# A two-layer SCNN block: the fourth group's rows of layer 1 move between the two column scans, and the hand-over from rows to columns goes from tile to tile

## The chip, the cores and the metric

The kernel runs on one core of a Trainium2 chip. The metric is device time in microseconds (us) of one execution; a time "of the kernel" below is the median of three executions.

## The reference

The input `x` is an image batch of shape (32, 48, 64, 128): 32 images, 48 channels, 64 rows, 128 columns, all in f32. There are two layers, and each adds a scan to its input: `x = x + scnn(groupnorm(x))`. The normalization takes 16 groups of 3 channels per image. The scan is a spatial recurrence in four directions, one after another:

```python
def step(w, b):                       # w: 48 x 48 channels x 5 taps
    def f(carry, inp):
        nxt = inp + conv1d(carry, w, b)    # padding 2, along the line
        return nxt, nxt
    return f
# D: down the 64 rows (carry = a row of 128 columns), weights down_w
# U: up the rows of D, again with down_w
# R: right over the 128 columns of U (carry = a column of 64 rows), right_w
# L: left over the columns of R, left_w
```

A step needs the whole result of the step before it, so 2 x 63 row steps and 2 x 127 column steps of one image can't be done at the same time. Only different images are independent.

## The kernel before

**Tiling.** The 32 images are four groups of eight. A *row phase* runs the down and up scans of one group: 63 + 63 steps. A *column phase* runs the right and left scans of a *pair* of groups: 127 + 127 steps. With two layers there are eight row phases and four column phases, 2024 steps. TensorE runs them strictly one after another, in the order of the list `PHASES`; each entry is (kind, layer, group or pair), and k is a phase's place in the list, counted from 0. Before the change the end of the list is rows of layer 1 for groups 1, 2 and 3, then columns of layer 1 for pair 0 and for pair 1.

A step (function `step`, line 741) is nine 128x128 matmuls into three PSUM banks, and after each bank an add on VectorE (line 750) that puts bias and input to it and writes the new row or column into SBUF. The tiles of a step are named step_, layer, group or pair, and way: step_10r is layer 1, pair 0, right; step_13d is layer 1, group 3, down. A phase is called 10r, 13d and so on below.

**Memory.** SBUF holds an `arena` with three slots and four *stage* tiles, and a region `early` with weights. A row phase uses two slots (rows 0 to 31 and 32 to 63); which two alternates with the phase's number. A column phase works in quarters of 32 columns, three at a time: quarter 0 is spilled to DRAM after use and comes back for the left scan, and quarter 3 takes its place (`spill_unit`). Two more tiles, `spare_tiles`, lie on the region `early`, the first of them on the down weights.

**Two layouts.** In a row phase a partition is (column modulo 8, channel), in a column phase it is (row modulo 8, channel); both in three sets of 128. Going from rows to columns is a transposition between partitions. It is done by way of DRAM: `move_rows` writes rows to the buffers `ups` (line 589, in the trace `upa` and `upb` by layer), and `load_unit` (line 231's `dma`) reads them column-wise. Where a column phase comes straight after the row phase of its pair's second group, the last rows are on the critical path: this is called a *seam* (`follows`). There are two seams before the change: rows 01 to columns 00 and rows 03 to columns 01. At a seam the rows 0 and 1, which are finished last, are written and read separately, the reads on GpSimd's queue. `hold_queues` (the tile `pin`) makes SyncE's and ScalarE's queues wait until the first column is taken, so that the loads of the second quarter come behind.

**Row phases.** `plan_rows` loads a group's 64 rows in four batches of 16, and applies the normalization to each (`scale_rows`: 24 activations on ScalarE, line 614). Both have times of their own; behind a column phase the loads start 28, 12 steps before and 4, 20 steps after the phase's first step, the scalings 13 before and 3, 19, 35 after.

**Results of layer 1.** In the left scan a finished quarter's six units are handled one by one in `plan_cols`: the residual is loaded into a tile (`load_residual`, from the DRAM buffer `mid`, on ScalarE's queue), added on GpSimd (line 673), permuted by GpSimd and ScalarE (lines 569 and 698), and stored. Quarters 3 to 0 follow in this order. The results of the first pair's quarters 2, 1 and 0 (`HELD`) are first kept in DRAM (`hold_result`, ScalarE's queue) and later moved to the output (`let_result`, SyncE's queue). The residual for result n+2 into the tile of result n-2 (with four tiles) is issued after result n's copies:

```python
if u >= 2 and u - 2 + n < len(direct):
    at(t + 4.6, load_residual, k, *direct[u - 2 + n][1:], tiles[(u - 2) % n])
```

**The order is written by hand.** `at(t, fn, ...)` puts a call on an agenda at a time t counted in steps; `in_order` ties the instructions so that each engine keeps that order. DMAs go out on the queues of SyncE, ScalarE and GpSimd, each in order: an instruction that waits holds up all that stands behind it on its engine. The DMAs of SyncE and ScalarE share eight semaphores in turn, so that a DMA may also wait until the one eight before it in the program, on either queue, has landed.

Of the kernel before, what the change touches and what calls it, by code (L numbers as in the profile page):

```python
# [43 lines left out]
E8 = 8  # L44
FULL = 128
NG = E8 * C // FULL
NQ = 4
# [31 lines left out]
def weight_runs():  # L79
# [31 lines left out]
    ("cols", 0, 1),  # L111
    ("rows", 1, 1),
    ("rows", 1, 2),
    ("rows", 1, 3),
    ("cols", 1, 0),
    ("cols", 1, 1),
)

# [2 lines left out]
def kernel(  # L121
# [8 lines left out]
    nc = tc.nc  # L130
    B, _, H, W = x.shape
# [5 lines left out]
    RUN = KQ * GB  # L137
# [34 lines left out]
    spare_tiles = [early[:, i * UNIT : (i + 1) * UNIT] for i in range(2)]  # L172
# [38 lines left out]
        for half in range(2)  # L211
    }

    def by_row(t, e, h0, h1):


        t = t.rearrange("c (i q a e n) -> e a c i q n", i=E8, q=NQ, a=NH, e=E8)[e, h0 // E8]
        return t[:, h0 % E8 : h0 % E8 + h1 - h0].rearrange("c i q n -> c (i q) n")

    def lines(t, h0, h1):  # L220

# [8 lines left out]
    def dma(dst, src, queue=None):  # L230
        (queue or nc.sync).dma_start(dst, src)

    tail = {}

    def in_order(fn, *args):


        traced = nc.cur_bb.bb.instructions
        n = len(traced)
        fn(*args)  # L240
        for ins in traced[n:]:
            if ins.engine in tail:
                tc.add_manual_dep(
                    ins,
                    tail[ins.engine].name,
                    mybir.DependencyInfo(
                        mybir.DependencyClass.NoSync, mybir.DependencyReason.DATA
                    ),
                    reason="in_order",
                )  # L250
            tail[ins.engine] = ins

    def pieces(o):
# [332 lines left out]
    def row(k, h):  # L586
        return row_views(k)[h // HALF][:, :, h % HALF]

    def move_rows(k, h0, h1, to_dram):

        _, layer, g = PHASES[k]
        view = row_views(k)[h0 // HALF]
        t = (ups if to_dram else source)[layer][g]
        for h in range(h0, h1, E8):
            end = min(h1, h + E8)
            for o in range(NG):
                for e, c0, c1, p0 in pieces(o):
                    here = view[p0 : p0 + c1 - c0, o, h % HALF : h % HALF + end - h]
                    here = here.rearrange("p h (q n) -> p (h q) n", q=NQ)
                    there = by_row(t, e, h, end)[c0:c1]  # L600
                    if to_dram:
                        dma(there, here)
                    else:
                        dma(here, there)
# [25 lines left out]
    def quarter(k, j):  # L630
        return slot[slots(k)[j % 3]].rearrange("p (o s n) -> p s o n", s=2, o=NG)

    def load_unit(k, j, i, a0=0, a1=NH, e0=0, e1=E8, queue=None):


        _, layer, pair = PHASES[k]
        o, half = UNITS[i]
        part = slice(a0 * LINE, a1 * LINE)
        for e, c0, c1, p0 in pieces(o):
            if not e0 <= e < e1:  # L640
                continue
            dma(
                quarter(k, j)[p0 : p0 + c1 - c0, half, o, part],
                by_col(ups[layer][2 * pair + half], e, j)[c0:c1, part],
                queue,
            )

    def hold_queues(k):

# [170 lines left out]
    def at(t, fn, *args):  # L820
        agenda.append((t, len(agenda), fn, args))
# [31 lines left out]
    def plan_rows(k, t0, prev):  # L853
        if k == 1:
            ahead, scaled = (-34, -18, -3, 12), (-12, -2, 17, 33)
        elif prev == "cols":
            ahead, scaled = (-28, -12, 4, 20), (-13, 3, 19, 35)
        else:
            ahead, scaled = (-54, -43, 0, 11), (-22, -8, 16, 30)
        if k:  # L860
            for i in range(4):
                at(t0 + ahead[i], move_rows, k, i * LOAD, (i + 1) * LOAD, False)
                at(t0 + scaled[i], scale_rows, k, i * LOAD, (i + 1) * LOAD)

        cuts = list(range(0, H + 1, E8))
        following = PHASES[k + 1][0] == "cols"
        if following and follows(k + 1):
            cuts = [0, E8 // 4] + cuts[1:]
        for h0, h1 in zip(cuts, cuts[1:]):
            t = t0 + 2 * (H - 1) - h0  # L870
            if k == 0:
                t += 16 if h0 >= HALF else 68
            elif not following:
                t = t0 + 92 + 5 * (H - h1) / E8 + (34 if h1 <= HALF else 0)
            at(t, move_rows, k, h0, h1, True)
        at(
            t0 + H - 1,
            nc.gpsimd.tensor_copy,
            last.rearrange("p (o n) -> p o n", o=NG),
            row(k, H - 1),  # L880
        )

    def follows(k):

        _, layer, pair = PHASES[k]
        return PHASES[k - 1] == ("rows", layer, 2 * pair + 1)

    def plan_cols(k, t0, prev):
        _, layer, pair = PHASES[k]
        n = 2 * NG  # L890
# [3 lines left out]
        for i in range(n):  # L894
            if follows(k) and UNITS[i][1] == 1:
                other = nc.gpsimd
                at(t0 - 31 + i, load_unit, k, 0, i, 4, NH, 0, E8, other)
                at(t0 - 13 + i, load_unit, k, 0, i, 2, 4, 0, E8, other)
                at(t0 - 6 + i / n, load_unit, k, 0, i, 1, 2, 0, E8, other)
                at(t0 - 1.5, load_unit, k, 0, i, 0, 1, E8 // 4, E8, other)  # L900
                at(t0, load_unit, k, 0, i, 0, 1, 0, E8 // 4, other)
            else:
                early = 30 if after else 46 if k == 2 else 70
                at(t0 - early + 2 * i, load_unit, k, 0, i)
            if follows(k):
                queue = nc.scalar if i % 2 else nc.sync
                at(t0 + 1.5, load_unit, k, 1, i, 0, NH, 0, E8, queue)
            else:
                at(t0 + (3 if after else -24 + 2 * i), load_unit, k, 1, i)
            at(t0 + (38 if after else 8) + 2 * i, load_unit, k, 2, i)  # L910
            at(t0 + 33 + 2 * i, spill_unit, k, i, False)
            at(t0 + 50 + 2 * i, load_unit, k, 3, i)
        final = k == len(PHASES) - 1
        left = t0 + W - 1
        end = left + W - 1
        for i in range(n):

            t = left + 64 + 2 * i if layer == 0 else left + 39.5 + 4.5 * i
# [8 lines left out]
        if layer == 0:  # L927
            stats = ResultStatsV(f"r{2 * pair}"), ResultStatsA(f"r{2 * pair + 1}")
        tiles = [stage[:, i] for i in range(4)]
        if layer:  # L930
            tiles += spare_tiles[0 : 2 if final else 1]
        n = len(tiles)
        direct = [u for u in units if not (final and u[1] == 0)]

        for u, (t, j, i) in enumerate(direct):
            nat = tiles[u % n]
            o, half = UNITS[i]
            if u < n:
                soon = layer and u < 5
                at(left - 44 + 4 * u if soon else left + 16, load_residual, k, j, i, nat)  # L940
            if layer == 0:
                if u >= n:
                    at(direct[u - n][0] + 3, load_residual, k, j, i, nat)
                at(t, add_residual, k, j, i, nat)
                at(t + 4, keep_result, k, j, i)
                unit = quarter(k, j)[:, half, o]
                if half == 0:
                    for b in range(GB):
                        at(t + 5 + b, stats[0].take, j, o, unit, b)
                else:  # L950
                    at(t + 1, stats[1].take, j, o, unit)
            else:

                at(t, add_residual, k, j, i, nat)
                at(t + 2.5, permute_unit, k, j, i, nat, (nc.gpsimd, nc.scalar, nc.scalar))
                if final or j not in HELD:
                    at(t + 4.5, store_result, k, j, i, nat)
                else:
                    at(t + 4.5, hold_result, j, i, nat)
                if final and j == 1:  # L960
                    at(t + 4.7, load_residual, k, 0, i, last_tiles(k)[i])

                if u >= 2 and u - 2 + n < len(direct):
                    at(t + 4.6, load_residual, k, *direct[u - 2 + n][1:], tiles[(u - 2) % n])
        if layer == 0:
            t = units[-1][0] + 14
# [6 lines left out]
        if layer and not final:  # L973
            todo = [(j, half, e) for j in HELD for half in range(2) for e in range(E8)]
            for n, what in enumerate(todo):
                at(end + 63 + 1.9 * n, let_result, *what)
        if final:
            at(end + 4, last_results, k)

# [230 lines left out]
```

## Time and profile before

| | |
|---|---|
| runs of the kernel | 4333.52, 4343.96, 4350.06 us; median 4343.96 |
| profiled execution, own time | 4343.96 us; its span 4342.2 us |
| PE (TensorE) busy | 4066.5 us, 94% of the span, 36648 matmuls |
| DVE (VectorE) busy | 2165.5 us, 50% |
| ACT (ScalarE) busy | 1340.3 us, 31% |
| POOL (GpSimd) busy | 885.6 us, 20% |
| DMA | 680.12 MB, mean 157 GB/s |

"Busy" is the time in which an engine had an instruction at work; register, wait and DMA-issuing instructions are not counted. In a group's line the columns are: the source line, engine, operation, output and input with their shapes, the number of instructions, and behind the bar the busy time in us, the mean of one in ns, and the idle time of the engine just before them with what ended most of it. "PEclk" or "granted clock" is TensorE's clock as a share of full speed. In DMA lines the columns are the number of issues, the size of each and the median time from issue to landing.

### The profile page before, as it was taken

What the parts mean: (1) busy time and instruction counts of PE and PEld (TensorE: products, weight loads), DVE (VectorE), ACT (ScalarE), POOL (GpSimd) and SP (SyncE); (2) the same over time, 40 slices, a digit from 0 to 9 for tenths busy, and PEclk for the clock granted to TensorE, in tenths of its full rate; (3) what the DMA queues carried; (4) which work ended last, traced back from release to release, by engine and by line L of the source; (5) the groups of instructions that cost most, each with busy time, mean ns of one, the idle gap of its engine ahead of it and who ended that gap; (6) DMA issues with size and microseconds to landing.
All of it is one profiled execution on the core that took longest, in us unless ns stands there. A gap on an engine that the chain in (4) does not pass through costs nothing. (4 is left out here: it accounts for less than half of the span.)

```text
span 4342.2 us, 89984 instructions
## 1 busy us (share of the span) xinstructions
PE 4066.5 (94%) x36648; PEld 4036.5 (93%) x36648; DVE 2165.5 (50%) x6503; ACT 1340.3 (31%) x2662; POOL 885.6 (20%) x906
## 2 busy tenths in 40 slices
PE   3799998999999999989999999999997999989993
PEld 1699998999999999989999999999997999989992
DVE  6345444446654444444447654444443444444443
ACT  1584301526783556000006855403000002210122
POOL 4271011325323020010013410000000014520352
PEclk9899999999999999999999999999998999999996
DMA  8589799848999979579218979759049409999999
GB/s 211 112 215 163 108 163 188 224 112 242 221 181 163 157 148 154 95 125 225 48 27 272 199 144 156 108 90 179 3 67 179 118 13 244 247 250 167 156 211 182
DMA packets 2116733, 680.12 MB, mean 157 GB/s; under 512 B 2005440, under 2 KB 2056160, under 8 KB 2076384
## 3 DMA queue, kind: packets, MB, share of 16 engines
q1 hardware_dynamic: 2015904, 581.64, 69.2%
q10 hardware_dynamic: 97216, 86.44, 9.5%
q0 software_dynamic: 3200, 6.30, 0.6%
q8 instruction: 288, 4.72, 0.5%
q14 instruction: 125, 1.02, 0.1%
HBM read 397.38 MB, written 295.98 MB: 160 GB/s over the span
## 5 line engine op out<-in xcount | busy, mean ns | idle before, releaser
L614 ACT ACTIVATE arena<-arena,offset,scale 128x256 f32<-128x256 f32 (+2 forms) x816 | 575.7, 798 | 439.5 <-PE step_12u L741 116.8
L673 POOL TENSOR_TENSOR arena<-arena 128x2048 f32<-128x2048 f32 x80 | 363.0, 4553 | 1437.0 <-PE step_10l L741 501.6
L569 POOL COPY arena<-arena 96x256 f32<-96x256 f32 x448 | 264.8, 644 | 555.2 <-DMA arena<-in_x 445.4
L741 PE MATMUL step_10r<-arena,early 128*128 128x128 f32 x2286 | 254.0, 275 | 37.7 <-DVE arena L750 29.0
L741 PEld LDWEIGHTS step_10r<-arena,early 128*128 128x128 f32 x2286 | 253.6, 187 | 38.0 <-DVE arena L750 29.2
L512 ACT ACTIVATE early<-arena 128x256 f32<-128x256 f32 x192 | 129.6, 675 | 482.0 <-DMA arena<-xin 319.5
L741 PE MATMUL step_11r<-arena,early 128*128 128x128 f32 x2286 | 251.5, 274 | 15.2 <-DVE arena L750 15.2
L741 PEld LDWEIGHTS step_11r<-arena,early 128*128 128x128 f32 x2286 | 251.0, 185 | 15.6 <-DVE arena L750 15.6
L741 PE MATMUL step_01r<-arena,early 128*128 128x128 f32 x2286 | 251.1, 274 | 14.5 <-DMA arena<-upa 14.5
L741 PEld LDWEIGHTS step_01r<-arena,early 128*128 128x128 f32 x2286 | 250.9, 185 | 14.8 <-issue 14.7
L741 PE MATMUL step_00r<-arena,early 128*128 128x128 f32 x2286 | 250.9, 273 | 14.5 <-DMA arena<-upa 14.5
L741 PEld LDWEIGHTS step_00r<-arena,early 128*128 128x128 f32 x2286 | 250.6, 185 | 14.8 <-issue 14.8
L741 PE MATMUL step_00l<-arena,wleft 128*128 128x128 f32 x2286 | 249.1, 272 | 0.0
L741 PEld LDWEIGHTS step_00l<-arena,wleft 128*128 128x128 f32 x2286 | 248.6, 184 | 0.0
L741 PE MATMUL step_10l<-arena,wleft 128*128 128x128 f32 x2286 | 248.5, 272 | 0.0
L741 PE MATMUL step_11l<-arena,wleft 128*128 128x128 f32 x2286 | 248.5, 272 | 0.0
L741 PE MATMUL step_01l<-arena,wleft 128*128 128x128 f32 x2286 | 248.4, 272 | 0.0
L741 PEld LDWEIGHTS step_10l<-arena,wleft 128*128 128x128 f32 x2286 | 248.4, 184 | 0.0
L741 PEld LDWEIGHTS step_11l<-arena,wleft 128*128 128x128 f32 x2286 | 248.4, 184 | 0.0
L741 PEld LDWEIGHTS step_01l<-arena,wleft 128*128 128x128 f32 x2286 | 248.4, 184 | 0.0
L698 ACT COPY arena<-arena 128x256 f32<-128x256 f32 x172 | 99.6, 656 | 409.7 <-POOL arena L673 180.9
L240 ACT COPY early<-arena 128x1 f32<-128x1 f32 x2 | 0.4, 191 | 707.0 <-DVE arena L750 547.5
(189 smaller groups left out, 7175.8 us busy)
## 6 DMA issues: line engine op xcount, KB each, us to landing
arena<-in_x SPq DMA_DIRECT2D x24, 1536.0 KB, 12.1
xin<-arena SPq DMA_DIRECT2D x96, 384.0 KB, 4.7
arena<-xin SPq DMA_DIRECT2D x96, 384.0 KB, 8.7
mid<-arena SPq DMA_DIRECT2D x96, 384.0 KB, 7.9
arena<-mid SPq DMA_DIRECT2D x192, 192.0 KB, 4.2
upb<-arena SPq DMA_DIRECT2D x192, 192.0 KB, 4.0
arena<-upb SPq DMA_DIRECT2D x96, 384.0 KB, 12.2
arena<-xin SPq DMA_DIRECT2D x186, 192.0 KB, 4.2
```

What stands on the lines that cost most here:

```text
L240: fn(*args)
L512: nc.scalar.activation(junk[:, 0:n], view[:, b], AF.Identity, accum_out=self.sum[:, i, j : j + 1])
L569: copy(dst[:, r, q], src[:, r0 + r, q])
L614: nc.scalar.activation(args[0], args[0], AF.Identity, bias=args[2], scale=args[1])
L673: eng.tensor_tensor(unit, unit, nat, ALU.add)
L698: copy(by_w(perm)[:, a], src[:, a])
L741: nc.tensor.matmul(part(whole(ps[o])[0:m], -s), weights[:, i, at : at + m], part(src(i), s), start=seen[o] == 1, stop=seen[o] == left[o],)
```

## The change

- In `PHASES` the rows of the fourth group of layer 1 (group 3) stand behind the first pair's columns of layer 1. So the end of the list is rows 11, rows 12, columns 10, rows 13, columns 11, and the second pair's columns of layer 1 become a third seam.
- At all seams the last eight rows go from tile to tile. For rows 7 to 0, the pieces of the first quarter's columns are sent from the row tile straight into the column tile (`send_row`): half of them (column modulo 8 under 4) as each row is done, the other half behind the last row (`send_rest`). That is 94 DMAs of 48 partitions or fewer, 128 B each, alternately on ScalarE's and SyncE's queue. Rows 8 to 15 go to DRAM with their first quarter's columns alone eight steps before the end, and are loaded on GpSimd's queue as before. Whole rows 0 to 15 go to DRAM 1.3 steps after the end, behind the others; GpSimd's loads of rows 0 to 7 are gone. An added tie (`together`) keeps the DMAs of both queues in one order.
- Columns of layer 1 other than the last have four tiles for results in place of five, and the first residuals are all loaded at `left + 16`; the last columns keep six tiles, without the early loads.
- The moves of the held results to the output (`let_result`) start 12 steps after the first pair's columns in place of 63, one every 4 steps in place of 1.9, those from the 27th on 70 steps later.

```diff
@@ PHASES
     ("rows", 1, 2),
+    ("cols", 1, 0),
     ("rows", 1, 3),
-    ("cols", 1, 0),
     ("cols", 1, 1),
@@ in_order
+            if ins.engine in queues and "DMA" in ins.opcode:
+                if fn in together and "queue" in tail:
+                    tc.add_manual_dep(
+                        ins,
+                        tail["queue"].name,
...
+                tail["queue"] = ins
             tail[ins.engine] = ins
@@ move_rows (nq=1: the first quarter's columns alone)
-    def move_rows(k, h0, h1, to_dram):
+    def move_rows(k, h0, h1, to_dram, nq=NQ):
...
+                    if nq == NQ:
+                        here = here.rearrange("p h (q n) -> p (h q) n", q=NQ)
+                    else:
+                        here = here[:, :, 0:RUN]
@@ new
+    def send_row(k, h, wanted):
+
+        here = row(k - 1, h)
+        for e, c0, c1, o, p0 in PIECES:
+            if e not in wanted:
+                continue
+            for i, d0, d1, to, q0 in PIECES:
+                a, b = max(c0, d0), min(c1, d1)
+                if i != h or a >= b:
+                    continue
+                turns[0] += 1
+                dma(
+                    quarter(k, 0)[q0 + a - d0 : q0 + b - d0, 1, to, e * RUN : (e + 1) * RUN],
+                    here[p0 + a - c0 : p0 + b - c0, o, 0:RUN],
+                    nc.scalar if turns[0] % 2 else nc.sync,
+                )
+
+    def send_rest(k, wanted):
+
+        for e in wanted:
+            for h in range(E8 - 1, -1, -1):
+                send_row(k, h, (e,))
@@ plan_rows
-        if following and follows(k + 1):
-            cuts = [0, E8 // 4] + cuts[1:]
+        seam = following and follows(k + 1)
+        if seam:
+            cuts = cuts[2:]
+            end = t0 + 2 * (H - 1)
+            at(end - E8, move_rows, k, E8, 2 * E8, True, 1)
+            for h in range(E8 - 1, -1, -1):
+                at(end - h, send_row, k + 1, h, range(0, E8 // 2))
+            at(end, send_rest, k + 1, range(E8 // 2, E8))
+            at(end + 1.3, move_rows, k, 0, E8, True)
+            at(end + 1.3, move_rows, k, E8, 2 * E8, True)
@@ plan_cols
-                at(t0 - 1.5, load_unit, k, 0, i, 0, 1, E8 // 4, E8, other)
-                at(t0, load_unit, k, 0, i, 0, 1, 0, E8 // 4, other)
...
-        if layer:
-            tiles += spare_tiles[0 : 2 if final else 1]
+        if final:
+            tiles += spare_tiles
...
-                soon = layer and u < 5
-                at(left - 44 + 4 * u if soon else left + 16, load_residual, k, j, i, nat)
+                at(left + 16, load_residual, k, j, i, nat)
...
-                at(end + 63 + 1.9 * n, let_result, *what)
+                at(end + 12 + 4 * n + (70 if n > 25 else 0), let_result, *what)
```

More of the change, by code (lines that the diff above doesn't have):

```diff
@@ L212, with by_row @@
     }
-    def by_row(t, e, h0, h1):
+    def by_row(t, e, h0, h1, nq):
         t = t.rearrange("c (i q a e n) -> e a c i q n", i=E8, q=NQ, a=NH, e=E8)[e, h0 // E8]
-        return t[:, h0 % E8 : h0 % E8 + h1 - h0].rearrange("c i q n -> c (i q) n")
+        t = t[:, h0 % E8 : h0 % E8 + h1 - h0]
+        return t.rearrange("c i q n -> c (i q) n") if nq == NQ else t[:, :, 0]
     def lines(t, h0, h1):
@@ L233 @@
     tail = {}
+    queues = (nc.sync.engine, nc.scalar.engine)
+    together = []
     def in_order(fn, *args):
@@ L250, in in_order @@
                 )
+            if ins.engine in queues and "DMA" in ins.opcode:
[3 more added lines that the diff above has]
+                        tail["queue"].name,
+                        mybir.DependencyInfo(
+                            mybir.DependencyClass.NoSync, mybir.DependencyReason.DATA
+                        ),
+                        reason="together",
+                    )
+                tail["queue"] = ins
             tail[ins.engine] = ins
@@ L598, in move_rows @@
                     here = view[p0 : p0 + c1 - c0, o, h % HALF : h % HALF + end - h]
-                    here = here.rearrange("p h (q n) -> p (h q) n", q=NQ)
-                    there = by_row(t, e, h, end)[c0:c1]
+                    there = by_row(t, e, h, end, nq)[c0:c1]
+                    if nq == NQ:
+                        here = here.rearrange("p h (q n) -> p (h q) n", q=NQ)
+                    else:
+                        here = here[:, :, 0:RUN]
                     if to_dram:
@@ L646, in load_unit @@
             )
+    turns = [0]
+    def send_row(k, h, wanted):
[12 more added lines that the diff above has]
+                    nc.scalar if turns[0] % 2 else nc.sync,
+                )
+    def send_rest(k, wanted):
+        for e in wanted:
+            for h in range(E8 - 1, -1, -1):
+                send_row(k, h, (e,))
+    together += [send_row, send_rest]
     def hold_queues(k):
```

## The prediction

> **What bounds the kernel now.** I read the page's busy times, then TensorE's groups by line, then what SyncE's queue waited for. The names: step_10r is layer 1, pair 0, right; step_13d is layer 1, group 3, down.
>
> ```profile
> L741 PE MATMUL step_10r<-arena,early 128*128 128x128 f32 x2286 | 254.0, 275 | 37.7 <-DVE arena L750 29.0 <-DMA upb<-arena 8.7
> L741 PE MATMUL step_11r<-arena,early 128*128 128x128 f32 x2286 | 251.5, 274 | 15.2 <-DVE arena L750 15.2
> L741 PE MATMUL step_01r<-arena,early 128*128 128x128 f32 x2286 | 251.1, 274 | 14.5 <-DMA arena<-upa 14.5
> L741 PE MATMUL step_00r<-arena,early 128*128 128x128 f32 x2286 | 250.9, 273 | 14.5 <-DMA arena<-upa 14.5
> L741 PE MATMUL step_10l<-arena,wleft 128*128 128x128 f32 x2286 | 248.5, 272 | 0.0
> L741 PE MATMUL step_11d<-arena,early 128*128 128x128 f32 x1134 | 128.3, 276 | 6.7 <-DMA mid<-arena 4.7 <-issue 2.0
> ```
>
> TensorE steps one after another; a scan of 127 column steps takes 248.5 us when nothing is late, so 1.956 us a step, and a row scan 124.6. Excess is idle time plus busy time over that: 10r 37.7+5.5 = 43.2; 11r 15.2+3.0 = 18.2; 01r 17.1 and 00r 16.9, the two seams. These 95.4 us are what the change can reach.
>
> ```profile
> SPq L231 <- DMA early<-mid: 182.5, 2, 181.6
> ```
>
> That is SyncE's queue between 2990 and 3330 us. It stood 181.6 us behind a residual load into the fifth tile, which lies on the down weights and had to wait for the last row scan. So the rows of group 3 went out only after 3216, and the second quarter of 10r came late.
>
> ```profile
> 1938.00:1952.00 14.00, 2.11 (x10) 2.10 (x11) 0.00 (x0) 0.00 (x0) 5.57 (x12) 0.50 0.51 94
> 1235.00:1241.00 6.00, 5.10 (x24) 5.13 (x25) 1.66 (x5) 5.78 (x16) 0.00 (x0) 0.50 1.25 168
> early<-taps SPq DMA_DIRECT2D x5, 6.0 KB, 1.6
> upb<-arena SPq DMA_DIRECT2D x27, 192.0 KB, 4.0
> pin<-arena SPq DMA_DIRECT2D x1, 0.5 KB, 8.2
> arena<-mid ACTq DMA_DIRECT2D x8, 384.0 KB, 13.4
> L673 POOL TENSOR_TENSOR arena<-arena 128x2048 f32<-128x2048 f32 x80 | 363.0, 4553 | 1437.0 <-PE step_10l L741 501.6
> L614 ACT ACTIVATE arena<-arena,offset,scale 128x256 f32<-128x256 f32 (+2 forms) x816 | 575.7, 798 | 439.5 <-PE step_12u L741 116.8
> ```
>
> Two windows (the eighth column is the granted clock), four rows of DMA issues from four stretches (KB each, us to landing), two groups of the page.
>
> **10r, first pair's columns.** The fifth tile and the early loads go, so SyncE is free and the 43.2 goes. What is late next: the second quarter's 20 loads queue from 24 steps (47 us) ahead and are due 62 us after the start, against the 44 us that the same loads took in 01r. I take 1 (0 to 5).
>
> **11r and the boundary columns to columns.** 18.2 goes; a seam and a boundary columns to rows come instead.
>
> **13d, rows after columns.** ScalarE now holds, in this order, the copies of quarter 1's results 1 to 4, 24 scalings of rows 0 to 15, results 5 and 6, 24 of rows 16 to 31, results 1 and 2 of quarter 0, 24 of rows 32 to 47, results 3 to 5, 24 of rows 48 to 63. A batch of scalings is 24 x 0.8 = 19.2 us, and its rows can't be stepped before. With four tiles the residual of result n+2 is issued after the copies of result n: (4.55 add + 2.9 copies + 2 issue + 13.4 landing)/2 = 11.5 us a result; transfers are crowded here (235 to 250 GB/s in 3690 to 3780), which makes it up to 12.5. In us from the boundary (the first step of 13d is 0): quarter 2 of the left scan is finished 123 us before it; counted from its first result, the fourth of quarter 1 is nine intervals on, its add at -20 to -11, its copies done at -12 to -4, rows 0 to 15 scaled at +7 to +15. Only then is the sixth residual issued, since it stands behind those scalings on ScalarE: 25 us until its copies are done (2 + 13.4 + 4.55 + 2.9, and a little for the neighbour), and 19.2 for the second batch: +51 to +59. Row 16 is due at 16 x 1.98 = 32, so 20 to 28 late. The third batch ends 31 later (+82 to +90, due 63): no later. The fourth waits for a residual issued behind it, 24 + 19: +125 to +133, due 95: 30 to 38 late. I take 33, and 2.6 for the clock after it: 36. Bounds: 10.4 (11d, rows after columns in layer 0: 6.7 + 3.7) and 58 (residuals landing in 20, the slowest in 3740 to 3770). I take the upper half since 11d's results needed no permutes and no held copies. SyncE's moves of held results to the output, which start 51 steps (some 100 us) earlier than now and come every 7.9 us in place of 3.7, sit behind row loads that are due later, and are free; uncovered a move costs its own 6.6.
>
> **Each seam.** Gone: two passes through DRAM, 14.5 idle. Added: 47 tile-to-tile moves (48 partitions x 128 B) under the last eight rows, 47 behind them, ten issues on POOL's path for rows 8 to 15. The trace has no such move; nearest are the weight loads, 1.6 to 1.8 us to landing and 0.465 apart on one queue, so 0.233 on two; upper bound 4.0 (192 KB stores); nothing makes them cheaper than nothing. I take 1.7. Row 0's first move issues when DVE's first output is done (0.4 before TensorE ends), lands 1.4 after, 0.5 for the start as now: 2.2 idle, and half of the 2.6 that a seam's slower clock costs now (17.1 - 14.5), as 2.6 of idle in 02d at 1234 was followed by a clock of 0.50: 1.5 in all. The other 47 issue in 11 us and land by +13.6, due +15.1: hidden.
>
> But they, the pin (8.2), and then 20 row stores now stand on SyncE ahead of the second quarter's loads: +1, +12, +20.5, then 20 x 0.875 = 17.5; ScalarE's half waits until +38. The loads start at +32 and need 36 to 38, so land near +69; column 32 is due at 2.2 + 31 x 1.956 + 1.2 = +64. Now they have 14 us to spare. So a new wait of 5 (0 if the pin doesn't hold the stores, 14 if the stores take 1.0 and the loads 43 as now), and 2.6 for the clock. Sum 2.2 + 1.5 + 5 + 2.6 = 11.3 (4 to 25).
>
> The Trainium skill, "TensorE: Matmul & The Clock Gate", Part 1, lets the clock fall only after an idle window of about 3.4 us; the 02d row above differs, and the row decides. By the rule each seam would be 1.5 us cheaper, 4 us in all. "DMA: Bandwidth & Descriptors", Bandwidth, speaks against the change: transfers under 64 KB are bound by descriptors, with some 2.0 us fixed; an estimate by it is 12 us for 47 moves, eight in flight, one more than the rows give.
>
> **Sum.** Removed 43.2 + 18.2 = 61.4. Added 1 + 36 + 11.3 = 48.3. Old seams 2 x (17 - 11.3) = 11.4. Gain 24.5. The profiled execution is 4343.96 (span 4342.2), which is also the median of the three shown (4333.5 to 4350.1): 4319.5. The end, 75.9 us from the last matmul to the end of the span, is the same code.
>
> **Rivals.** A: the fourth group's rows cost what 11d's do (10.4) and the seams 5: gain 61.4 - 16.4 + 24 = 69, so 4275. For it: the held copies land in 5.6 to 8.5 us at 3640. Against: 12 to 15 from 3690 on.
> B, slower: the moves between tiles land in 4.6 us instead of 1.7. Eight may be out at once, so 47 take 27 us, the last lands at +32.5, due +15: 17 more waiting, and the second quarter keeps its 5: 32 a seam, 3 x 21 = 62 more, 4382. It decides from 3.0 us (no gain) to 4.0 (4366). Against it: small moves land in 1.6.
> C: the change doesn't free 10r, because another load blocks SyncE's queue there: 43.2 stays, 4362. Against it: in the changed order nothing before the spill waits on ScalarE's queue.
>
> **Numbers.** The forecast 0.52 (own range 4300 to 4336), A 0.27, B 0.09, C 0.12. A measurement here tells 0.5% (21.7 us) from no change: faster means under 4322.2, over half of the forecast's case and all of A: 0.55; slower over 4365.7: 0.09 from B and C; 0.36 between. Range: A's side down to 4272, up to 4358.
>
> **What would show it.** 10r at 249 to 254 with no idle, SyncE never over 100 us on a ScalarE load: right. step_13d with some 30 idle released by ScalarE L631: right; under 12: A. At the seams 2 to 3 idle and a second wait of some 5 at column 32. Idle within columns 4 to 7, or moves landing over 3 us: B. 10r with 30 or more idle: C and a wrong prediction.

## The result: slower, and the profile after

The changed kernel takes 4387.81 us (median of four runs, 4379.59 to 4393.66) against 4342.53 of the kernel before in the same series. The ratio is 1.0104, with a 95% interval of 1.0075 to 1.0132: it is slower by about one per cent. The forecast was a gain, 4319.5, with a range that ended at 4358. The profiled execution of the changed kernel took 4379.59 us, 35.6 more than that of before (4343.96); the decomposition below compares these two.

The same groups as before the change, from the page of the changed kernel and its answer on TensorE's groups by line:

```profile
L785 PE MATMUL step_10r<-arena,early 128*128 128x128 f32 x2286 | 248.4, 272 | 0.0
L785 PE MATMUL step_13d<-arena,early 128*128 128x128 f32 x1134 | 134.2, 284 | 43.4 <-DVE arena L794 22.1 <-issue 21.3
L785 PE MATMUL step_00r<-arena,early 128*128 128x128 f32 x2286 | 253.9, 275 | 20.5 <-DMA arena<-upa 14.6 <-DMA arena<-arena 5.1 <-DVE arena L794 0.7
L785 PE MATMUL step_01r<-arena,early 128*128 128x128 f32 x2286 | 252.4, 274 | 22.8 <-DMA arena<-upa 14.4 <-DMA arena<-arena 6.0 <-DVE arena L794 2.3
L785 PE MATMUL step_11r<-arena,early 128*128 128x128 f32 x2286 | 253.1, 274 | 25.5 <-DVE arena L794 16.5 <-DMA arena<-arena 8.9
```

The first line is the gain: 10r runs without a pause, as forecast. The second is the fourth group's rows behind the first pair's columns: 43.4 us idle, and 134.2 busy in place of 124.6. The last three are the seams. Each has a first wait for a move from tile to tile (`arena<-arena`, 5.1, 6.0 and 8.9 us) and a second, larger one, some 14 us, for the second quarter's loads (`arena<-upa` from DRAM; in 11r the page names VectorE, whose add waits for the same load, and 16.5 there includes 2.5 us of small waits).

Measured from the matmuls' start and end times in the trace, a phase's cost is the idle time ahead of it plus its length over an undisturbed one (248.45 for a right scan, 124.6 for a down scan):

| | forecast | measured |
|---|---|---|
| 10r: 291.68 to 248.45 | -42.2 | -43.2 |
| 11r's wait at column 64 (18.2 before) | -18.2 | -18.2 |
| 13d: 20.6 ahead of it, 156.97 long | +36 | +53.0 |
| third seam, 11r: 8.91 ahead, 269.65 long | +11.3 | +30.1 |
| old seams: 17.0 and 17.2 before, 25.9 and 26.7 after | -11.4 | +18.4 |
| sum | -24.5 | +40.1 |

The rest of the program gives -4.5 between the two executions (35.6 - 40.1), which is within what two runs of one kernel differ by.

### The profile page after: what moved, and what is told of

It is laid out like the page before. It is cut to its first block, busy times and chain, and to the rows that moved or that the text cites. A ratio compares the mean times of both kernels' runs of the same rounds, so it can differ in the third digit from the quotient of the medians.

```text
span 4377.7 us, 90553 instructions
## 1 busy us (share of the span) xinstructions
PE 4077.0 (93%) x36648; PEld 4043.8 (92%) x36648; DVE 2167.0 (50%) x6503; ACT 1339.0 (31%) x2663; POOL 891.2 (20%) x916
## 5 line engine op out<-in xcount | busy, mean ns | idle before, releaser
L717 POOL TENSOR_TENSOR arena<-arena 128x2048 f32<-128x2048 f32 x84 | 381.1, 4550 | 1577.0 <-PE step_10l L785 451.8
L785 PE MATMUL step_11r<-arena,early 128*128 128x128 f32 x2286 | 253.1, 274 | 25.5 <-DVE arena L794 16.5
L785 PEld LDWEIGHTS step_01r<-arena,early 128*128 128x128 f32 x2286 | 251.6, 186 | 23.6 <-DVE arena L794 17.2
L785 PE MATMUL step_00r<-arena,early 128*128 128x128 f32 x2286 | 253.9, 275 | 20.5 <-DMA arena<-upa 14.6
L785 PEld LDWEIGHTS step_00r<-arena,early 128*128 128x128 f32 x2286 | 253.0, 186 | 21.4 <-DVE arena L794 15.9
L785 PE MATMUL step_01l<-arena,wleft 128*128 128x128 f32 x2286 | 248.4, 272 | 0.0
L785 PE MATMUL step_10r<-arena,early 128*128 128x128 f32 x2286 | 248.4, 272 | 0.0
L785 PEld LDWEIGHTS step_11l<-arena,wleft 128*128 128x128 f32 x2286 | 248.4, 184 | 0.0
L785 PEld LDWEIGHTS step_01l<-arena,wleft 128*128 128x128 f32 x2286 | 248.4, 184 | 0.0
L785 PEld LDWEIGHTS step_10r<-arena,early 128*128 128x128 f32 x2286 | 248.4, 184 | 0.0
L742 ACT COPY arena<-arena 128x256 f32<-128x256 f32 x192 | 110.7, 653 | 391.2 <-POOL arena L717 199.3
## 6 DMA issues: line engine op xcount, KB each, us to landing
arena<-in_x SPq DMA_DIRECT2D x24, 1536.0 KB, 11.5
```

Of the source, the lines that this page charges most:

```text
L717: eng.tensor_tensor(unit, unit, nat, ALU.add)
L742: copy(by_w(perm)[:, a], src[:, a])
L785: nc.tensor.matmul(part(whole(ps[o])[0:m], -s), weights[:, i, at : at + m], part(src(i), s), start=seen[o] == 1, stop=seen[o] == left[o],)
```

## The experiments

Unless said otherwise, times are medians and ratios are to the kernel before, measured in the same series, with a 95% interval in brackets. In the edits, "..." marks lines left out, here and below. Waits and costs of a phase are read from the trace of one execution of each kernel.

### The seams: the old hand-over in the new order

```diff
-            at(end - E8, move_rows, k, E8, 2 * E8, True, 1)
-            for h in range(E8 - 1, -1, -1):
-                at(end - h, send_row, k + 1, h, range(0, E8 // 2))
-            at(end, send_rest, k + 1, range(E8 // 2, E8))
...
+            cuts = [0, E8 // 4] + cuts[1:]
...
+                at(t0 - 1.5, load_unit, k, 0, i, 0, 1, E8 // 4, E8, other)
+                at(t0, load_unit, k, 0, i, 0, 1, 0, E8 // 4, other)
```

> The changed order of phases with the old hand-over at its three seams. Theory (the moves from tile to tile cost more than the DRAM path they replace): each seam goes back to 17, from the 25.9, 26.7 and 30.1 of the changed kernel (idle ahead of the columns' first step plus the right scan's length over 248.45), 31.7 in all: 4356, between 4350 and 4362. Rival (the third seam is dear for its place behind the results of layer 1, not for its form): only the first two give back 18, the third keeps some 30: 4369.

Measured (run `old_seams`): 4355.86 us, ratio 1.0028 (1.0016 to 1.0040). The seams cost 17.6, 17.4 and 18.1 in its trace, 53.1 together against 82.7. The third seam is no dearer than the others with the old hand-over, so its place is not the cause; the new hand-over is. It costs some 30 us more on the three seams.

### The four tiles alone

```diff
-        if layer:
-            tiles += spare_tiles[0 : 2 if final else 1]
+        if final:
+            tiles += spare_tiles
...
-                soon = layer and u < 5
-                at(left - 44 + 4 * u if soon else left + 16, load_residual, k, j, i, nat)
+                at(left + 16, load_residual, k, j, i, nat)
```

> The kernel before with one edit: columns of layer 1 other than the last have four result tiles and no early residual loads; the old order of phases and the old seams stay. Theory (SyncE's queue was blocked by the fifth tile's load alone): 10r falls from 291.7 to 249 to 254 and the time by 38 to 43: 4300 to 4305. Rival (with four tiles the results come later, and the next columns' wait at column 64, 15.2 now, grows by as much): 4325 to 4345.

Measured (run `four_tiles`): 4303.66 us, ratio 0.9904 (0.9884 to 0.9924), faster than both kernels. Its groups:

```profile
L741 PE MATMUL step_10r<-arena,early 128*128 128x128 f32 x2286 | 248.4, 272 | 0.0
L741 PE MATMUL step_11r<-arena,early 128*128 128x128 f32 x2286 | 251.4, 274 | 17.1 <-DVE arena L750 17.1
L741 PE MATMUL step_13d<-arena,early 128*128 128x128 f32 x1134 | 124.6, 273 | 0.0
```

The gain at 10r, 43 us, comes from this one edit and needs no new order of phases. The other gain that was forecast, the wait at column 64 of 11r, needs the new order: here it stays (17.1). With old_seams this also prices the new order: 4355.86 - 4303.66 = 52 us lost, which is 13d's 52.4 there, and the third seam's 18.1 in place of 11r's 20.0 (17.1 and 2.9 of slower clock).

### The second wait of a seam: ten loads ahead

```diff
-                queue = nc.scalar if i % 2 else nc.sync
-                at(t0 + 1.5, load_unit, k, 1, i, 0, NH, 0, E8, queue)
+                if UNITS[i][1] == 0:
+                    at(t0 - 24 + 2 * i, load_unit, k, 1, i)
+                else:
+                    queue = nc.scalar if i == 3 else nc.sync
+                    at(t0 + 1.5, load_unit, k, 1, i, 0, NH, 0, E8, queue)
```

> The changed kernel with the second quarter's loads of the first group (10 of 20, its rows were done long before) issued 24 steps ahead of the seam. Theory (the wait at column 32 is the 20 loads standing behind 94 moves, the pin and 20 stores): the ten left start at the same +47 us, take half of 40 and land at +67, due +73: the wait of 14.0 to 14.6 at column 32 falls to 0 to 3 at each seam, and 2.6 of clock with it: 4387.8 - 3 x (12 to 17) = 4337 to 4352. Rival (the moves' own landing and a crowded DMA set it, not the number of loads): over 8 stays at each, 4365 or more.

Measured (run `half_ahead`): 4374.65 us, ratio 1.0065 (1.0046 to 1.0085). The wait at column 32 is gone at all three seams, as the theory has it, but the time is the rival's, since the first step's wait rose to 15.9, 14.9 and 22.3:

```profile
L785 PE MATMUL step_01r<-arena,early 128*128 128x128 f32 x2286 | 252.6, 274 | 17.4 <-DMA arena<-arena 14.9 <-DVE arena L794 2.5
```

The ten loads ahead stand among the row stores on SyncE's queue, and the stores and moves behind them go out later: in 01r's seam the first move goes 3.3 us ahead of the last row's end, in the changed kernel 11.1. The seams cost 20.0, 21.5 and 28.3, together 12.9 less than in the changed kernel, and the median fell by 13.2. So what stands in the queue ahead of the loads does set the second wait; but a load taken out of it there comes back ahead of the first step.

### The first wait: all moves on one queue

```diff
-                    nc.scalar if turns[0] % 2 else nc.sync,
+                    nc.sync,
```

> The changed kernel with all 94 moves of a seam on SyncE's queue. Theory (an issue holds its own queue for 0.6 us, so two queues give one in 0.32): the 47 moves under the rows take 28 us in place of 15.5, so the columns' first step waits some 14 us more (20 in place of 6.0 before 01r), the rest ends another 15 later and column 32 waits some 28 more less the 14: three seams cost 80 to 90 more, 4470. Rival 1 (the moves' spacing is a limit that both queues share): unchanged, 4380 to 4395. Rival 2 (one queue alone issues every 0.465 as the weight loads did): +6.5 and +7 a seam, 4428.

Measured (run `one_queue`): 4484.47 us (one run), near the theory's 4470; the first steps of the three seams wait 19.2 to 19.5 us in its trace, where the theory had 20. The timeline of 01r's seam in the changed kernel (start, length, queue, number of moves), of a stretch in which the issues of both queues follow one another without other waits:

```profile
1945.48 11.51 SPq L232 DMA_DIRECT2D arena<-arena  x18
1945.82 11.51 ACTq L232 DMA_DIRECT2D arena<-arena  x18
```

and a stretch of the run with one queue:

```profile
1974.69 15.56 SPq L232 DMA_DIRECT2D arena<-arena  x24
```

On either, one move holds its queue for 0.64 us (11.51/18) or 0.65 (15.56/24); two queues together give one in 0.32. The moves landed near the forecast's 1.7 (medians):

```profile
arena<-arena ACTq DMA_DIRECT2D x18, 6.0 KB, 1.8
arena<-arena SPq DMA_DIRECT2D x18, 6.0 KB, 1.8
arena<-arena ACTq DMA_DIRECT2D x17, 2.0 KB, 2.0
arena<-arena SPq DMA_DIRECT2D x15, 2.0 KB, 1.8
```

(the changed kernel, 1927 to 1960 us: KB each, us to landing). So the size that was wrong is the spacing of the issues, not the landing. One queue alone needs as long for a move as each of two, so it is the issue on a queue that takes the time, and no limit that both share. Why a move holds its queue longer than a weight load (0.465) was not tested. The Trainium skill, "DMA: Bandwidth & Descriptors", section "Issuing engines are not separate DMA queues", says that issuing from several engines saves only the sequencers' time, "which is usually small relative to the DMA itself". Here it is not small: 0.64 of issue against 1.8 to 2.0 us to landing, and with 94 moves in a row the issue is what counts.

### Fewer rows from tile to tile

The kernel with the old order and four tiles (4303.7), with 47 moves a seam in place of 94:

```diff
+            at(end - E8 // 2, move_rows, k, E8 // 2, E8, True, 1)
-            for h in range(E8 - 1, -1, -1):
+            for h in range(E8 // 2 - 1, -1, -1):
                 at(end - h, send_row, k + 1, h, range(0, E8 // 2))
...
+                at(t0 - 3 + i / n, load_unit, k, 0, i, 0, 1, E8 // 2, E8, other)
```

> The old order of phases with four result tiles and held results at the old times (as four_tiles, 4303.7), and at its two seams rows 3 to 0 alone from tile to tile (47 moves), rows 4 to 7 through DRAM with their first quarter 4 steps ahead. Theory (a move takes 0.32 of issue, so a row of 5 to 7 moves per 1.98 us just keeps pace, and the backlog is the number of rows sent): no backlog, row 0's first moves go at +0.4 to +1.4 and land 1.7 later: the first step waits 3 to 5 in place of 14.4, the moves end at +10, the second quarter's 20 loads start near +37, need 40, due near +70: 5 to 9 at column 32. A seam costs 13 to 18 (17 the old way): 4296 to 4306. Rival (the backlog comes from waits for the stores of rows 8 to 15 on the shared queues and stays): first step over 7, 4306 or more.

Measured (run `four_rows`): 4307.56 us, ratio 0.9912 (0.9893 to 0.9931). The first step waits 4.9 and 4.6, inside the theory's 3 to 5; column 32 waits 9.2 and 13.1, more than its 5 to 9. A seam costs 20.2 and 21.8, more than the theory's 13 to 18 and no less than the old way. Then ten of the second quarter's loads on GpSimd's queue, right behind its last loads of the first quarter:

```diff
+                if UNITS[i][1] == 0:
+                    at(t0 + 0.5, load_unit, k, 1, i, 0, NH, 0, E8, nc.gpsimd)
```

> As four_rows, with ten of the second quarter's 20 loads (the first group's, ready long before) on GpSimd's queue right behind its last loads of the first quarter. Theory (column 32 waits for what stands in the queues of SyncE and ScalarE): ten loads left there, start near +37, need 20, land at +57, due +70: no wait at column 32, a seam costs 6 to 10 in place of 17: 4282 to 4292. Rival (the ten loads crowd the moves and the stores, as they did 24 steps ahead in half_ahead, where the first step's wait rose to 15 to 22): a seam stays at 14 or more, 4297 or more.

Measured (run `four_rows_pool`): 4301.76 us, ratio 0.9902 (0.9884 to 0.9919). No wait at column 32, but the first step waits 8.5 and 10.7, since the ten loads start 1.2 us behind the last row and the moves issued beside them land in 5 to 12 us; a seam costs 14.5 and 15.1, as the rival has it. Last, the same loads held back behind the third column step (a one-column copy on GpSimd, and the loads 3.3 steps after the start):

```diff
+            done = quarter(k, 0)[:, 0, 0, 3 * RUN : 3 * RUN + 1]
+            at(t0 + 3.2, nc.gpsimd.tensor_copy, junk[:, BN - 2 : BN - 1], done)
...
-                    at(t0 + 0.5, load_unit, k, 1, i, 0, NH, 0, E8, nc.gpsimd)
+                    at(t0 + 3.3, load_unit, k, 1, i, 0, NH, 0, E8, nc.gpsimd)
```

> As four_rows_pool, but the ten loads on GpSimd's queue stand behind a one-column copy there that needs the third column step, so that they start at some +14 us instead of +1.2, behind the moves from tile to tile. Theory (the loads crowded the moves in four_rows_pool: the last moves landed 8 to 12 us after their issue in place of 1.7): the first step waits 4.6 to 4.9 again, as in four_rows, the moves end at +10 to +12, no wait of over 2 at column 32: a seam costs 8 to 10 in place of 17: 4285 to 4291. Rival (with the half ahead, the other ten loads and the row stores still take as long, since the DMA engines and not the queues set it): column 32 waits 5 or more, 4297 or more.

Measured (run `four_rows_held`): 4308.78 us, ratio 0.9919 (0.9902 to 0.9936). The first step waits 4.7 and 4.6 again, but now the 20 row stores take longer to go out, and column 32 waits 6.5 and 5.8, as the rival has it:

```profile
1940.73 37.57 SPq L232 DMA_DIRECT2D upa<-arena  x20
```

37.57 us for the stores (timeline, second seam), against 24.66 in the changed kernel. A seam costs 17.8 and 15.5. None of the three is told apart from four_tiles by its median.

### 13d: scalings on VectorE

The 96 scalings of group 3's rows on VectorE, one every 0.4 step, in place of ScalarE:

```diff
-                at(t0 + scaled[i], scale_rows, k, i * LOAD, (i + 1) * LOAD)
+                if k == len(PHASES) - 2:
+                    spread(
+                        t0 + scaled[i], scale_by_vector(k, i * LOAD, (i + 1) * LOAD), 0.4
+                    )
+                else:
+                    at(t0 + scaled[i], scale_rows, k, i * LOAD, (i + 1) * LOAD)
```

> The changed kernel with the scalings of group 3's rows in layer 1 (96 of 128x256) on VectorE, one every 0.4 step, in place of ScalarE. Theory (13d waits for scalings queued on ScalarE behind copies of results): its 53.0 (20.6 before its first step, 156.97 in place of 124.6) falls to 0 to 12; some steps get longer by a scaling ahead of an add: 4335 to 4350. Rival (the rows themselves come late, since their loads wait for the results' slots): 30 or more stays, 4365 or more.

Measured (run `scale_vector`): 4389.79 us, ratio 1.0103 (1.0085 to 1.0122): no gain, as the rival has it. The waits moved ahead of the boundary (10l took 269.53 in place of 248.85) and 13d took 161.28; together 57.4 lost in place of 53.0. VectorE's own waits from 3440 to 3620 us (line, what it waited for, us in total, times, longest):

```profile
DVE arena L644 <- DMA arena<-mid: 18.7, 4, 10.2
```

L644 is the new scaling; it waited for the rows themselves. The rest of the 57 us this run doesn't divide, since the scalings (0.52 us each) now stand among the steps' adds. It shows that ScalarE's order alone is not the cause: a scaling waited up to 10.2 us for its rows with no copy in front of it.

### 13d: less traffic, the same order

```diff
-        dma(held[j, half][o], perm, nc.scalar)
+        dma(held[j, half][o][:, 0 : UNIT // 8], perm[:, 0 : UNIT // 8], nc.scalar)
...
-        src = held[j, half].rearrange("o p (a b n) -> (o p a) b n", a=NH, b=GB)
+        src = spill[2][0:NG].rearrange("o p (a b n) -> (o p a) b n", a=NH, b=GB)
```

> The changed kernel with each held result cut to an eighth of its columns on its way to DRAM (18 x 0.875 MB less from 3340 to 3620, 15.8 of 58.6 MB), and the later moves to the output read another buffer of the same shape; the instructions and their order on every engine stay. Theory (13d's 53 is DMA volume: 59 MB at 209 GB/s are 280 us): 75 us of DMA time go, 13d loses under 12 in place of 53.0: 4340 to 4350. Rival (the order on ScalarE, each residual 13 us and each batch of scalings 19 whatever the volume): 40 or more stays, 4375 or more.

Measured (run `thin_holds`): 4345.42 us, ratio 1.0006 (0.9992 to 1.0019), 42 less than the changed kernel. This kernel leaves out seven eighths of each held result, so it doesn't give the output; it serves for its time alone. Its 13d:

```profile
L785 PE MATMUL step_13d<-arena,early 128*128 128x128 f32 x1134 | 130.5, 279 | 8.1 <-DVE arena L794 8.1
```

13d's cost fell from 53.0 to 14.0 (138.57 long, no wait ahead of it): slightly over the theory's 12, far under the rival's 40. One stretch of both kernels, the changed one first (length, busy us of PE, PEld, DVE, ACT, POOL, then granted clock, DMA share, GB/s):

```profile
3340.00:3620.00 280.00, 236.54 (x2081) 234.95 (x2080) 111.49 (x347) 122.94 (x186) 114.36 (x72) 0.92 1.09 209
```

```profile
3340.00:3620.00 280.00, 271.86 (x2436) 270.73 (x2435) 130.40 (x406) 123.51 (x186) 114.89 (x73) 0.98 1.04 173
```

ScalarE works 123 us of 280 in both, with the same instructions in the same order; the DMA engines are busy throughout. In the changed kernel 58.56 MB go through in this stretch, 48.32 in the other (10 MB less and not 15.8, since later transfers moved up into it). The holds and ScalarE's residual loads, with KB each and the median time to landing, the changed kernel first:

```profile
held<-arena ACTq DMA_DIRECT2D x18, 1024.0 KB, 6.0
arena<-mid ACTq DMA_DIRECT2D x34, 384.0 KB, 9.1
```

```profile
held<-arena ACTq DMA_DIRECT2D x18, 128.0 KB, 4.7
arena<-mid ACTq DMA_DIRECT2D x34, 384.0 KB, 6.8
```

The residual loads, whose size is the same, landed sooner too. That 39 of 13d's 53 us go with the bytes of the holds, with every instruction in its place, is shown by this run; what the other 14 are was not tested. The DMA engines' busy share is no measure of it: it is near 1 in both.

### Two that tested smaller statements

The moves of held results at their old times, in the changed kernel:

```diff
-                at(end + 12 + 4 * n + (70 if n > 25 else 0), let_result, *what)
+                at(end + 63 + 1.9 * n, let_result, *what)
```

> The changed kernel with the moves of held results to the output at their old times (63 steps behind the first pair's columns, every 1.9). Theory after the first four runs (from 3300 to 3615 us the DMA engines are busy all the time, 58.6 MB from 3340 to 3620 at 209 GB/s, and 13d waits for them): the four moves that stood on SyncE from 3539 to 3554 ahead of the last row loads go, and the third wait of 13d, 11.6, falls to 0 to 5: 4376 to 4383. Rival (the prediction's statement that they are free there): 13d stays at 177 to 179 from the end of 10l, 4388.

Measured (run `let_old`): 4423.64 us, ratio 1.0181 (1.0162 to 1.0200). Both missed. 13d falls only from 53.0 to 50.3, and the third wait of it from 11.6 to 9.8: within 3 us, the moves were free in 13d, as the prediction said. But at the old times they come between the row stores, and even between the moves, of the third seam, and 11r's first step waits 50.5 in place of 8.9:

```profile
L785 PE MATMUL step_11r<-arena,early 128*128 128x128 f32 x2286 | 256.0, 276 | 64.6 <-DMA arena<-arena 51.3 <-DVE arena L794 13.3
```

So this edit belongs to the new order and saves it 36 us.

The kernel before with four tiles, but the first four residuals early:

```diff
-            tiles += spare_tiles[0 : 2 if final else 1]
+            tiles += spare_tiles
...
-                soon = layer and u < 5
+                soon = layer and not final and u < 4
```

> The kernel before with four result tiles in the first pair's columns of layer 1 (as in the run four_tiles) but the first four residuals early, from 44 steps ahead of the left scan, and none early in the last columns. Theory (DMA volume in the second half of 10l sets 11r's wait at column 64, 17.1 in four_tiles): 4 MB, 19 us at 209 GB/s, move into idle DMA time, the wait falls to 0 to 8 and the time to 4287 to 4297. Rival (quarter 0's results can't start before the scan gives them, so what was loaded early doesn't matter): 14 or more stays, 4304.

Measured (run `four_early`): 4298.83 us, ratio 0.9893 (0.9874 to 0.9912), not told apart from four_tiles; 11r's wait at column 64 is 16.7, so the rival is right. What sets that wait is left open; the forecast needed only that it goes with the new order, and it did.

## Why the prediction was wrong

**What bounds the kernel, and the fifth tile: right.** SyncE's queue stood behind the fifth tile's load, and without it 10r has no pause (248.4 busy, 0.0 idle). Rival C is out. The 1 us kept for the second quarter's loads was not needed.

**Each seam: the step that failed.** The forecast was 11.3 (4 to 25), measured 25.9, 26.7 and 30.1: 48.6 of the 64.6 us by which the sum of the phases missed. The terms of its sum, with what they measured:

- *The spacing of the moves.* "0.465 apart on one queue, so 0.233 on two" was taken from weight loads, which issue in less. It is 0.64 and 0.32. "47 issue in 11 us" is then 15, and the other 47 end at +21.7 instead of +12. The estimate from the Trainium skill, 12 us, is short as well; its 2.0 us fixed stand in "DMA: Bandwidth & Descriptors" under "Anatomy of one DMA — SWDGE (gpsimd) path", fitted on DMAs that GpSimd issues, and these moves are issued by SyncE and ScalarE.
- *The first step's wait, 2.2.* "Row 0's first move issues when DVE's first output is done" left out what stands in front of it. The 47 moves under the last eight rows need 15 us of the two queues and the rows give 15.8, but they start late, behind the stores of rows 8 to 15. In 01r's seam the first goes at 11.1 us ahead of the last row's end (1938.70), in 11r's at 9.2, and row 0's move for column 1 goes at +4.3 and +7.2; it lands 1.7 later, and the first step starts at +6.0 and +8.9. The 47 moves on ScalarE's queue take 32.8 us from 1927.61 on, the 47 on SyncE's 31.8 from 1928.61. With four rows sent in place of eight the wait is 4.6 to 4.9. In 11r's seam a move of a held result on SyncE stands among the stores, and let_old showed several of them to be costly there; that it is all of the 3 us between 01r and 11r was not tested.
- *The wait at column 32, 5, with 14 named as its far end.* The chain was right, its start was late, and the sum over it slipped. This is SyncE's queue in 01r's seam:

```profile
1957.04 3.40 SPq L232 DMA_DIRECT2D arena<-arena  x4
1960.85 0.34 SPq L232 DMA_DIRECT2D pin<-arena  x1
1961.24 24.66 SPq L232 DMA_DIRECT2D upa<-arena  x20
1986.01 43.06 SPq L232 DMA_DIRECT2D arena<-upa  x21
```

The moves end at +21.7, 9.7 late. From there the pin and the 20 stores take 25.6, against 8.5 and 17.5 in the forecast, so this link was right as a whole, and the loads start at +47.3. The forecast's own steps lead to +38 (20.5 and 17.5); its +32 doesn't follow from them, and from +38 the same chain gives a wait of 11 at column 32 in place of 5. In the old hand-over the stores of the last rows are on the path to the first step, but then the loads start at once. Here is the old one, in the run old_seams (the last row ends at 1929.98, so the loads start at +18.0):

```profile
1947.56 0.34 SPq L232 DMA_DIRECT2D pin<-arena  x1
1948.01 47.74 SPq L232 DMA_DIRECT2D arena<-upa  x21
```

The change took 8.5 us off the first step of 01r and put 29 us of moves and stores in front of the second quarter, where the old way had 14 to spare.

- *The clock.* The two waits together cost 4.0 to 5.5 us of slower clock (in 00r 269.23 - 248.45 - 0.69 - 14.59 = 5.5; in 01r 4.0). The sum had 1.5 + 2.6 = 4.1 (half of 2.6 is 1.3, where it took 1.5): right, or short by little.

**13d: the mechanism was half of it, the size short.** Forecast 36 (10.4 to 58), measured 53.0, inside the bounds. Read from the trace for each batch of 16 rows (us; "due" is when the steps could have used it, 16 steps apart from the end of 10l, without the earlier waits):

| batch | loads issued | landed | scaled | due | in thin_holds: landed, scaled, due |
|---|---|---|---|---|---|
| 0 | 3377.7 to 3440.6 | 3451.4 | 3474.0 to 3491.8 | 3469.8 | 3438.4, by 3470.4, 3471.5 |
| 1 | 3444.1 to 3484.8 | 3496.4 | 3507.4 to 3525.5 | 3501.4 | 3483.9, by 3500.5, 3503.2 |
| 2 | 3491.1 to 3537.1 | 3545.0 | 3550.0 to 3567.9 | 3533.1 | 3521.7, by 3538.3, 3534.8 |
| 3 | 3554.6 to 3595.0 | 3598.3 | 3591.4 to 3614.7 | 3564.7 | 3561.7, by 3578.2, 3566.5 |

Batch 0 lay in SBUF 18 us ahead of the boundary and waited for ScalarE, which first had to make the copies of a result: this is the prediction's mechanism, and the batch was done at +21 in place of +7 to +15, because a result took 13.2 us (3346.1 to 3464.6 in nine) in place of 11.5 to 12.5. What had grown was not the landing of the residuals (9.1 us in the median, 13.4 in the sum) but their issue: the three or four loads of one held ScalarE's queue for 2.6 to 12.6 us from 3380 to 3470, where the sum had 2. Batches 2 and 3 are another case: their rows landed 12 and 34 us after they were due, so no earlier scaling could have had them in time. The last batch sets 13d's cost: it was done 50 us after it was due (3614.7 against 3564.7), of which 34 had passed when its rows landed, and the slower clock behind the wait (0.92 from 3615 to 3650) brings the 50 to some 53. The forecast's fourth batch was 30 to 38 late, by a residual issued behind it. The forecast let ScalarE alone decide and took the rows' loads on SyncE for punctual. A batch's 20 loads were issued over 40 to 63 us, where 20 at the 0.875 that the prediction took for a row store make 17.5. In thin_holds, with the same order, everything is 13 to 37 us earlier.

Behind both stands one resource, as thin_holds shows for 39 of the 53 us: the DMA engines, which are busy for all of 280 us. The prediction noted the crowding and priced it as a longer landing of one residual; it didn't add up what has to pass: some 18 results with a residual and a hold of 1 MB each, 12.6 MB of rows, 3 of spilled units and some 7 to the output, 58.56 MB from 3340 to 3620. That is 280 us at the 209 GB/s measured there, and still 234 to 249 at the 235 to 250 that the trace of before showed, while the last rows were due 225 us after 3340. Not all of it has to pass ahead of the rows, so this is no price, but it says that the stretch was full before a chain was priced in it. The Trainium skill, "DMA: Bandwidth & Descriptors", section "Issuing engines are not separate DMA queues", states that the DMAs of all issuing engines run on the same 16 DMA engines and interleave; the window with a share of 1.09, and the rows that landed 13 to 37 us sooner by SyncE's queue when the holds on ScalarE's queue were cut, agree with it.

**The rivals.** A (rows cheap, seams 5) is out. B's number, 4382, is near the result and its sign is right, but its cause is not: moves landed in 1.8 to 2.0 us (medians), not 4.6, so the nearness is luck. Its place is partly right: waits of 0.7 to 2.3 within columns 4 to 7 were there, and with the issues twice as far apart, in one_queue, they were 2.2 to 8.5; and a loss of 48.6 us over the forecast's seams came by the queues that B named. B varied the landing alone; the other term that was borrowed from the weight loads, the spacing, was kept as a fact without a far end.

**The clock's rule.** The prediction preferred the trace's row (slower clock after 2.6 us idle) to the 3.4 us of the Trainium skill ("TensorE: Matmul & The Clock Gate", Part 1). The first waits of the seams were 5.1 to 8.9 us, longer than both, so nothing in them tells the two apart. Shorter waits speak for the row, without giving a bound: in thin_holds the granted clock is 0.50 from 3537.63 us on, 0.3 us behind a wait of 2.41 in 13d, while in the changed kernel it is 1.00 behind one of 2.33 in 01r (1962.7 to 1966).

## What to carry to other kernels

A transfer's time to landing and its time on the issuing queue are two prices, and for the 94 small transfers here the second decided: count issues per queue against the time under which they should hide, and add what already stands in that queue. When work moves off the critical path into a queue, find the next load behind it and its due time; here 8 us saved at the first step came back as 14 at column 32. Before two streams that each fit are put into the same stretch, add up their bytes and divide by the rate that the trace shows there: four_tiles, which moves nothing into the crowded stretch, keeps the gain at 10r with a small edit, and none of the kernels here is told apart from it as faster.

## What the runs showed of the hardware

Moves of 2 to 6 KB from one SBUF tile to another took 0.64 us of their queue each, whether one queue issued or two, and landed 1.8 to 2.0 us after issue (medians); with ten loads of up to 384 KB beside them they landed in 5 to 12. A DMA stream of packets nearly all under 512 B ran at 209 GB/s with the DMA engines shown busy all the time, and in thin_holds, with smaller holds in it, at 173 with a busy share as near 1.
